# Seven block products of a hybrid layer in another order: three copied by ScalarE and three sums on VectorE instead of one and five, one block summed by TensorE

## The chip, the cores and the metric

The kernel runs on one core of one Trainium2 chip. The metric is the device time of one execution in microseconds (us); the kernel before has a median of 2258.8 us over three runs (2258.38 to 2259.35). A lower time is better.

## What is computed

All data are FP32. A residual stream `x` of 1024 tokens by 512 goes through four layers, each with a layer norm ahead of it and an addition to `x` behind it:

```python
x = x + block_sparse_linear(layernorm(x))   # 512 x 512, 32x32 blocks masked
x = x + ffn(layernorm(x))                   # silu(x Wg) * (x Wu) @ Wd, int4-like weights, 1792 wide
x = x + mixer(layernorm(x))                 # state-space mixer, 2 sequences of 512 tokens
x = x + ffn(layernorm(x))                   # the same FFN again
```

In the mixer an input projection gives a gate `g` and an inner signal `x`, each 8192 wide, the shared matrices B and C (8 groups, 128 wide each) and a step size `dt` for each of 128 heads. A causal convolution of 4 taps and SiLU follow for `x`, B and C. A chunked scan computes, for each head, a masked score matrix times the inputs inside a chunk of 128 tokens, and the states carried from chunk to chunk. The result plus a skip term is normalised by its mean square, multiplied by SiLU(g) and projected back to 512.

## The kernel before, in words

**Products of two by two blocks.** Every large projection is cut into 2x2 blocks: two tiles of 128 output channels by two halves of 512 tokens, with the 512 inputs in two halves. Four output blocks of 128x512 would need eight block products; a scheme of the Strassen-Winograd kind does with seven. `left_sides` (L166) makes sums of the weights (`s1`, `s2`, `s3`, `s4`) on GpSimd; the sums of the activations (`t1` to `t4`) are made once for all in `tq` and in `xn_t` (L152 to L164; `last_quarter`, L164, overwrites a block of `xn_t` with `t3`, `third_quarter` makes `t4`).

`seven` (L177 to L227) is a Python generator with seven yields: each step issues one block product and what belongs to it, and the caller issues other work between the steps. One block product is the inner function `product` (L185): two FP32 matmuls of 128x128 by 128x512, of which TensorE (PE in the profile) runs two passes each, so four entries in the trace. The four output blocks are sums of the seven products. Part of a sum is made by TensorE itself, which adds a product to what already stands in a PSUM bank; part is made on VectorE (DVE), from a bank and an SBUF tile. Three PSUM banks, `x`, `y` and `z`, serve one `seven`. The order before is:

1. `x = a11 b11`; ScalarE (ACT) copies it to an SBUF tile, `c21` (L202).
2. `y = s2 t2`; DVE: `c12 = c21 + y` (L206).
3. `z = s1 t1`.
4. `y += s3 t3` on TensorE; DVE: `c22 = c21 + y` (L211), `c22 += z` (L212); output (1,1).
5. `x += a12 b21` on TensorE; output (0,0) straight from the bank.
6. `y += a22 t4`; DVE: `c21 + y` (L220); output (1,0).
7. `z += s4 b22`; DVE: `c12 + z` (L225); output (0,1).

With `in_place` the last two sums are written back into their bank, where `done` reads them. There are 96 such calls: 24 in the two FFNs (gate with tag `proj`, up with tag `yo`; `done` is a SiLU on ACT or a multiply on DVE), 32 in `x_front` (`proj`, in place; `done` is `conv`, which puts one ACT instruction, L732, and three DVE taps, L735, into a list that `drain` issues later), 8 in `group` (B and C of a group, in place, `done` again `conv`), and 32 in `g_front` (not in place; `done` only notes the tile, and its SiLU, L750, comes later as "later").

**Phases of the mixer.** The 64 channel tiles go two at a time through phases `ph` 1 to 32. A phase projects the tiles of the next step (`x_front`, then `g_front`), transposes the present ones (`tokens`: `x_tr` on PE, L828, and the product `x_dt` on DVE, L832), computes the scores of heads (`half_scores` and `back_scores`, each eight pieces a phase: four Relu, L893, an Exp, L900, an Exp, L903, all ACT; then a multiply by `gm` on DVE, L901, which waits in a list until `flush`; and a multiply on GpSimd, L907), the states (`both_states`), the scan (`half_scan`: `py` on PE, L920 and L929; the skip term L940 and the gating L943 on DVE) and projects an older phase back (`outs`, L957 with the sum L969; half of it by another scheme of seven products, `out_seven`, L1022 with the sum L1035). `squares` (L949 on ACT, L950 on GpSimd) collects the mean square. Seven of the 32 phases (3, 7, ... 27) also call `group` for new B and C; in those `g_front` uses only `proj` banks, elsewhere ("proj", "yo", "yo"). Ahead of phase 1 lies a set-up, written out by hand, with the first `x_front`, the step sizes (`step_sizes`), the cumulative sums (`decays`: `pacs`, `pa`, `pl`), the first group and the first `g_front`.

**What sets the order.** The order of the program is the order on PE, ACT and DVE; nothing reorders these queues. An instruction that waits holds up all behind it on its engine. GpSimd (POOL) and the DMA queue of SyncE (SP) follow the order of a scheduler. PSUM has three banks `proj`, three `yo`, two `tr`; the next owner of a bank waits for the last reader of the old one.

Of the kernel before, what the change touches and what calls it, by code (L numbers as in the profile page):

```python
# [27 lines left out]
CTG = NCT // G  # L28
# [5 lines left out]
PP = 2  # L34
# [3 lines left out]
def kernel(  # L38
# [138 lines left out]
    def seven(left, tag, tmp, done, in_place):  # L177


        a11, a12, s3, a22, s1, s2, s4 = left  # L180
        b11, t3, b21, b22, t1, t2, t4 = right

        def product(ps, a, b, start, stop):
            for kc in range(KH):
                nc.tensor.matmul(  # L185
                    ps,
                    lhsT=a[:, kc, :],
                    rhs=b[:, kc, :],
                    start=(start and kc == 0),
                    stop=(stop and kc == KH - 1),  # L190
                    skip_group_check=True,
                )

        tags = [tag] * 3 if isinstance(tag, str) else tag

        def bank(i):
            return psum.tile([P, SEQ], F32, tag=tags[i], name=f"{tags[i]}{i}", bufs=3)

        x = bank(0)
        c12, c21, c22 = tmp(0, 1), tmp(1, 0), tmp(1, 1)  # L200
        product(x, a11, b11, True, False)
        nc.scalar.copy(c21, x)  # L202
        yield
        y, z = bank(1), bank(2)
        product(y, s2, t2, True, False)
        nc.vector.tensor_add(c12, c21, y)  # L206
        yield
        product(z, s1, t1, True, False)
        yield
        product(y, s3, t3, False, False)  # L210
        nc.vector.tensor_add(c22, c21, y)  # L211
        nc.vector.tensor_add(c22, c22, z)  # L212
        done(1, 1, c22)
        yield
        product(x, a12, b21, False, True)
        done(0, 0, x)
        yield
        product(y, a22, t4, False, True)
        r = y if in_place else c21
        nc.vector.tensor_add(r, c21, y)  # L220
        done(1, 0, r)
        yield
        product(z, s4, b22, False, True)
        r = z if in_place else c12
        nc.vector.tensor_add(r, c12, z)  # L225
        done(0, 1, r)
        yield  # L227

    def stir(n):
# [440 lines left out]
    def mixer(waiting, step_args, loaded):  # L670

        with ExitStack() as st:
# [69 lines left out]
            def drain(n=None):  # L742

                n = len(taps) if n is None else min(n, len(taps))
                for f in taps[:n]:
                    f()
                del taps[:n]

            def silu(dst, src):
                nc.scalar.activation(dst, src, AF.Silu)  # L750
# [15 lines left out]
            def group_scores(made, shared, bs=range(2)):  # L766
                for b in bs:
                    b_t, c_t = made[b]
                    b_tok = grp.tile([P, NCH - 1, P], F32, tag=f"b_tok{b}", name="b_tok", bufs=1)
                    pt = psum.tile([P, NCH - 1, P], F32, tag="tr", name="b_tr")  # L770
                    for c in range(NCH - 1):
                        nc.tensor.transpose(pt[:, c, :], b_t[:, c * P : (c + 1) * P], ident)
# [8 lines left out]
                    shared.append((c_t, b_tok, gm))  # L781

            units = [(j, b) for j in range(PP) for b in range(2)]

# [301 lines left out]
            last_quarter()  # L1086
            third_quarter()
            next(steps)
            next(steps_dt)
            next(steps)  # L1090
            next(steps)
            next(steps_dt)
            drain(3)
            next(steps)
            next(steps)
            run(steps)
            exps = decays(1)
            groups[0] = []
            ces = []
            steps_bc, made = group(0, wbc, "yo")  # L1100
            next(steps_bc)
            exps()
            half_scores(0, 0, heads, ces)
            drain(3)
            next(steps_bc)
            drain(3)
            half_scores(1, 0, heads, ces)
            next(steps_bc)
            next(steps_bc)
            drain(3)  # L1110
            half_scores(2, 0, heads, ces)
            next(steps_bc)
            next(steps_bc)
            run(steps_bc)
            gate, later = g_front(wg, gts)
            next(gate)
            half_scores(3, 0, heads, ces)
            drain(3)
            next(gate)
            drain(3)  # L1120
            next(gate)
            for u in units:
                silu(xcs[u], xcs[u])
            next(gate)
            drain(3)
            for x in (*made[0], made[1][1]):
                silu(x, x)
            run(gate)
            for f in ces:
                f()  # L1130
            for dst, src in later:
                silu(dst, src)
            drain()
            silu(made[1][0], made[1][0])
            wx = load_pair(NCT + PP, NCT + PP + 1)


# [17 lines left out]

            for ph in range(1, n_ph + 1):
                front, last = ph < n_ph, ph >= 2
                if not front:

                    units = [(j, b) for b in range(2) for j in range(PP)]  # L1160
# [43 lines left out]
                mid = last and not final  # L1204
                if final:

                    gate_q = weights()
# [7 lines left out]
                tokens(1)  # L1215
                if made and last:
                    drain()
                    silu(made[1][0], made[1][0])
                if mid:
                    outs7 = out_seven(lefts, rights, ph == 2)  # L1220

# [15 lines left out]
                    next(steps)  # L1237
                    flush()
                    both_states(0)
                    o()  # L1240
                    next(steps)
                    o()
                    next(steps)
                    drain(3)
                    o()
                    back_scores(4)
                    next(steps)
# [52 lines left out]
                    for u in units:  # L1300
                        silu(xcs_new[u], xcs_new[u])
                    flush()
                    next(gate)
                    if not new_group:
                        drain(3)
                    run(gate)
                else:
                    next(steps)
                    if not last:
                        group_scores(made, groups[0], [0])  # L1310
                    else:
                        merge(1)
                    next(steps)
                    if not last:
                        group_scores(made, groups[0], [1])
                        made = None
                        flush()
                    else:
                        back_scores(2)
# [6 lines left out]
                        merge(3)  # L1326
                        back_scores(3)
                    next(steps)
                    flush()
                    if not last:  # L1330
                        back_scores(4)
                    both_states(0)
                    next(steps)
                    drain(3)
                    next(steps)
                    run(steps)
# [60 lines left out]
                    half_scores(1, c0, heads_new)  # L1397
                    if last:
                        next(gate)
                        for u in units:  # L1400
                            silu(xcs_new[u], xcs_new[u])
                        next(gate)
                    drain(3)
                    if last:
                        flush()
                    if final:
                        next(gate)
                        ups[0]()
                    run(gate)
                if not new_group:  # L1410
# [2 lines left out]
                    silu(dst, src)  # L1413
                if made:

                    for x in (*made[0], made[1][1]):
                        silu(x, x)
                    groups[(c0 + PP) // CTG] = []
                gts_old, gts, xcs, heads = gts, gts_new, xcs_new, heads_new


# [203 lines left out]
```

## Time and profile before

| | before |
|---|---|
| median of 3 runs | 2258.8 us (2258.38 to 2259.35) |
| profiled execution, span | 2256.4 us |
| granted clock of TensorE | 1.000 |
| ACT copies at L202 | 96, 564 to 613 ns |
| DVE sums at L206, L211, L212, L220, L225 | 5 x 96, 672 to 697 ns |

The profiled execution's span is 2.4 us under the median of the runs: it runs from the first to the last instruction and leaves out what lies around it. "Busy" is the share of the span in which an engine works; for an engine that does nothing but follow another it says little. The table of waits names who sat idle, for which instruction, and who ended it.

### The profile page before, as it was taken

The page shows a single profiled execution, that of the slowest core. Times are in us where ns is not written, and L with a number is a line of the kernel's source. Part 1 is how long each engine was busy: PE and PEld are TensorE (multiplying, and loading weights), DVE is VectorE, ACT ScalarE, POOL GpSimd, SP SyncE. Part 2 cuts the span into 40 slices and gives each one's busy share as a digit, 9 for nine tenths or more (in the row PEclk, how much of TensorE's full clock was granted, in tenths as well). Part 3 has the DMA queues.
Part 4 walks back from the last instruction along what each step waited for, and adds up shares of the span by engine and source line. Part 5 has one row for each costly group of instructions (what it writes and reads, how often), then busy time and mean ns, then how long its engine had stood idle before and what let it go on. Part 6 is the DMA issues. An engine that isn't in the chain of part 4 may idle for free.

```text
span 2256.4 us, 29331 instructions
## 1 busy us (share of the span) xinstructions
PE 2241.1 (99%) x10356; PEld 1340.5 (59%) x10356; DVE 1766.8 (78%) x3017; ACT 1166.2 (52%) x2474; POOL 1193.9 (53%) x1202
## 2 busy tenths in 40 slices
PE   9999999999999999999999999999999999999999
PEld 5445875556665665665566656656655666544468
DVE  5456558888888888888888888888888989865552
ACT  4111056756665665666566656656665665731100
POOL 3765023655655566566556555665665564536610
PEclk9999999999999999999999999999999999999999
DMA  6563021222222222222222222221222322337500
GB/s 196 191 202 108 24 70 61 80 66 76 74 69 73 76 75 85 65 77 82 66 77 70 71 75 74 77 84 60 82 76 67 111 66 75 122 103 232 196 10 28
DMA packets 145779, 201.53 MB, mean 89 GB/s; under 512 B 7136, under 2 KB 92000, under 8 KB 145632
## 3 DMA queue, kind: packets, MB, share of 16 engines
q1 hardware_dynamic: 145056, 198.61, 27.7%
q8 instruction: 82, 1.34, 0.2%
q10 hardware_dynamic: 576, 1.05, 0.1%
q14 instruction: 65, 0.53, 0.1%
HBM read 194.91 MB, written 4.72 MB: 88 GB/s over the span
## 4 chain that ended last, share of the span: by engine, by line
PE 95%; DVE 3%; ACT 1%; issue 0%; POOL 0%; DVEq 0%; ACTq 0%; POOLq 0%
PE proj L185 31%; PE yo L185 19%; PE po L957 11%; PE po L1022 8%; PE ffn_o L557 7%; PE py L920 5%; PE pst L849 4%; PE py L929 4%; PE x_tr L828 2%; PE pg L487 1%; PE bs_o L336 1%; PE pu L487 1%; PE pgm L779 1%; DVE xc L735 1%; PE ln_tr L142 0%; PE stir L233 0%
## 5 line engine op out<-in xcount | busy, mean ns | idle before, releaser
L907 POOL TENSOR_TENSOR ce<-ce,c_t 128x384 f32<-128x384 f32 x256 | 288.5, 1131 | 318.3 <-ACT ce L903 312.6
L185 PE MATMUL proj<-xn_t,w 128*128 128x512 f32 x824 | 384.6, 593 | 2.0 <-DVE gt L206 1.7
L893 ACT ACTIVATE m<-bc,acs 128x128 f32<-128x128 f32 x1024 | 324.8, 389 | 6.8 <-PE py L920 5.8
L185 PEld LDWEIGHTS proj<-xn_t,w 128*128 128x128 f32 x824 | 153.0, 190 | 155.8 <-issue 146.3
L957 PE MATMUL po<-wo,gt 128*128 128x512 f32 x528 | 238.2, 599 | 0.4 <-DVE y L940 0.4
L171 POOL TENSOR_TENSOR ws<-w 128x256 f32<-128x256 f32 x96 | 74.0, 771 | 308.7 <-DMA w<-in_win_t_dram 269.9
L901 DVE TENSOR_TENSOR m<-m,gm 128x512 f32<-128x512 f32 x256 | 227.6, 907 | 11.3 <-ACT m L900 10.4
L735 DVE SCALAR_TENSOR_TENSOR xc<-proj,cw,xc 128x511 f32<-128x511 f32 (+2 forms) x288 | 214.6, 746 | 6.6
L950 POOL TENSOR_TENSOR sq_acc<-sq_acc,y 128x512 f32<-128x512 f32 x128 | 175.8, 1377 | 76.7 <-ACT y L949 76.5
L185 PE MATMUL proj<-tq,ws 128*128 128x512 f32 x432 | 199.2, 592 | 0.0
L920 PE MATMUL py<-m,x_dt 128*64 128x128 f32 x2048 | 181.4, 276 | 0.1
L900 ACT ACTIVATE m<-m 128x512 f32<-128x512 f32 x256 | 161.3, 630 | 7.4
L957 PEld LDWEIGHTS po<-wo,gt 128*128 128x128 f32 x528 | 96.3, 190 | 109.7 <-issue 103.9
L185 PE MATMUL yo<-tq,ws 128*128 128x512 f32 x336 | 153.4, 599 | 0.4 <-ACT acs L715 0.4
L185 PE MATMUL yo<-xn_t,w 128*128 128x512 f32 x328 | 151.0, 592 | 0.0
L929 PE MATMUL py<-ce,state 128*64 128x128 f32 x1536 | 149.7, 273 | 0.0
L920 PEld LDWEIGHTS py<-m,x_dt 128*64 128x64 f32 x2048 | 122.5, 137 | 30.0 <-issue 14.4
L949 ACT ACTIVATE y<-y 128x512 f32<-128x512 f32 x128 | 76.5, 623 | 110.3 <-DVE gt L943 110.3
L969 DVE TENSOR_TENSOR x_sb<-x_sb,po 128x512 f32<-128x512 f32 x136 | 92.9, 685 | 48.9 <-PE po L957 47.2
L903 ACT ACTIVATE ce<-bc 128x384 f32<-128x384 f32 x256 | 129.8, 507 | 0.0
L245 POOL TENSOR_TENSOR w<-w,sf 128x1024 f32<-128x1024 f32 (+1 forms) x30 | 70.0, 2335 | 112.9 <-DVE w L244 87.2
L732 ACT ACTIVATE xc<-proj,cb,cw 128x512 f32<-128x512 f32 x96 | 74.2, 775 | 105.8 <-DVE proj L225 76.6
(229 smaller groups left out, 4491.7 us busy)
## 6 DMA issues: line engine op xcount, KB each, us to landing
bc<-acs_d SPq DMA_DIRECT2D x128, 512.0 KB, 3.8
w<-in_win_t_dram SPq DMA_DIRECT2D x64, 512.0 KB, 3.8
wo<-in_wo_t_dram SPq DMA_DIRECT2D x31, 512.0 KB, 4.0
wi<-in_down_w_dram SPq DMA_DIRECT2D x14, 512.0 KB, 3.9
zi<-in_down_z_dram SPq DMA_DIRECT2D x14, 512.0 KB, 4.7
sf<-in_down_s_dram SPq DMA_DIRECT2D x14, 512.0 KB, 4.3
wi<-in_gate_w_dram SPq DMA_DIRECT2D x13, 512.0 KB, 4.2
zi<-in_gate_z_dram SPq DMA_DIRECT2D x13, 512.0 KB, 5.3
```

What stands on the lines that cost most here:

```text
L185: nc.tensor.matmul(ps, lhsT=a[:, kc, :], rhs=b[:, kc, :], start=(start and kc == 0), stop=(stop and kc == KH - 1), skip_group_check=True,)
L557: nc.tensor.matmul(ps, lhsT=a[:, k, :], rhs=b(k), start=(start and k == 0), stop=(stop and k == KF - 1), skip_group_check=True,)
L735: nc.vector.scalar_tensor_tensor(dst[:, s:], ps[:, : SEQ - s], cw[:, t, 3 - s : 4 - s], dst[:, s:], ALU.mult, ALU.add)
L893: nc.scalar.activation(m[:, c, :], bc[:, hh, c * P : (c + 1) * P], AF.Relu, bias=acs[:, t, h : h + 1], scale=-1.0,)
L900: nc.scalar.activation(m, m, AF.Exp, scale=-1.0)
L901: mults.append(lambda: nc.vector.tensor_mul(m, m, shared[b][2]))
L907: nc.gpsimd.tensor_mul(ce, ce, c_t[:, P:].rearrange("p (c l) -> p c l", l=P))
L920: nc.tensor.matmul(py[hh * HD : (hh + 1) * HD, c * P : (c + 1) * P], lhsT=x_dt[:, c, hh, :], rhs=m[:, c, :], start=True, stop=(c == 0),)
L929: nc.tensor.matmul(py[hh * HD : (hh + 1) * HD, c * P : (c + 1) * P], lhsT=state[:, c - 1, hh, :], rhs=ce[:, c - 1, :], start=False, stop=True,
L950: nc.gpsimd.tensor_add(sq_acc[:, b, :], sq_acc[:, b, :], y)
L957: nc.tensor.matmul(po, lhsT=gts[j, b][:, c * P : (c + 1) * P], rhs=wo[:, j, :], start=(j == 0), stop=(j == PP - 1),)
L1022: nc.tensor.matmul(banks[k][:, c, :], lhsT=a[:, t], rhs=b, start=(start and c == 0), stop=stop, skip_group_check=True,)
```

## The change

The seven products stand in a new order with other sums:

1. `y = a11 b11`; ACT copies it to `m1`.
2. `z = s1 t1`; ACT copies it to `m3`.
3. `y += s2 t2` on TensorE; ACT copies the sum to `u2`.
4. `z += s4 b22`; DVE: `u2 + z`; output (0,1).
5. `y += s3 t3`; DVE: `m3 += y`; output (1,1).
6. `x = a12 b21`; DVE: `m1 + x`; output (0,0).
7. `y += a22 t4` on TensorE; output (1,0) straight from the bank.

So one copy and five sums become three copies and three sums; the number of products is the same. A product that adds to a bank must wait until the copy of that bank is done: 3 for `m1`, 4 for `m3`, 5 for `u2`; and 7 must wait for the sum of 5, which reads the same bank. The callers are fitted to the new order of outputs: some steps, drains, scores, squares and SiLUs stand elsewhere, and the list of a group's tiles becomes a dictionary, since B and C of the second sequence now come first.

```diff
-        x = bank(0)
-        c12, c21, c22 = tmp(0, 1), tmp(1, 0), tmp(1, 1)
-        product(x, a11, b11, True, False)
-        nc.scalar.copy(c21, x)
+        y = bank(0)
+        m1, m3, u2 = tmp(1, 0), tmp(1, 1), tmp(0, 1)
+        product(y, a11, b11, True, False)
+        nc.scalar.copy(m1, y)
         yield
-        y, z = bank(1), bank(2)
-        product(y, s2, t2, True, False)
-        nc.vector.tensor_add(c12, c21, y)
+        z = bank(1)
+        product(z, s1, t1, True, False)
+        nc.scalar.copy(m3, z)
         yield
-        product(z, s1, t1, True, False)
+        product(y, s2, t2, False, False)
+        nc.scalar.copy(u2, y)
+        yield
+        product(z, s4, b22, False, True)
+        r = z if in_place else u2
+        nc.vector.tensor_add(r, u2, z)
+        done(0, 1, r)
         yield
         product(y, s3, t3, False, False)
-        nc.vector.tensor_add(c22, c21, y)
-        nc.vector.tensor_add(c22, c22, z)
-        done(1, 1, c22)
+        nc.vector.tensor_add(m3, m3, y)
+        done(1, 1, m3)
         yield
-        product(x, a12, b21, False, True)
-        done(0, 0, x)
+        x = bank(2)
+        product(x, a12, b21, True, True)
+        r = x if in_place else m1
+        nc.vector.tensor_add(r, m1, x)
+        done(0, 0, r)
         yield
         product(y, a22, t4, False, True)
-        r = y if in_place else c21
-        nc.vector.tensor_add(r, c21, y)
-        done(1, 0, r)
-        yield
-        product(z, s4, b22, False, True)
-        r = z if in_place else c12
-        nc.vector.tensor_add(r, c12, z)
-        done(0, 1, r)
+        done(1, 0, y)
         yield
...
             next(steps)
+            next(steps)
             next(steps_dt)
             next(steps)
             next(steps)
             next(steps_dt)
+            next(steps)
             drain(3)
-            next(steps)
-            next(steps)
             run(steps)
...
             steps_bc, made = group(0, wbc, "yo")
             next(steps_bc)
             exps()
-            half_scores(0, 0, heads, ces)
             drain(3)
             next(steps_bc)
             drain(3)
-            half_scores(1, 0, heads, ces)
             next(steps_bc)
+            half_scores(0, 0, heads, ces)
             next(steps_bc)
             drain(3)
-            half_scores(2, 0, heads, ces)
             next(steps_bc)
+            half_scores(1, 0, heads, ces)
             next(steps_bc)
             run(steps_bc)
             gate, later = g_front(wg, gts)
             next(gate)
-            half_scores(3, 0, heads, ces)
+            half_scores(2, 0, heads, ces)
             drain(3)
             next(gate)
             drain(3)
             next(gate)
+            half_scores(3, 0, heads, ces)
+            drain()
+            next(gate)
+            next(gate)
             for u in units:
                 silu(xcs[u], xcs[u])
-            next(gate)
-            drain(3)
-            for x in (*made[0], made[1][1]):
+            for x in (*made[1], *made[0]):
                 silu(x, x)
             run(gate)
...
-                all_squares()
+                if not mid:
+                    all_squares()
...
                     next(steps)
+                    all_squares()
                     tokens(2)
                     tokens(3)
                     flush()
                     o()
                     next(steps)
-                    back_scores(2)
+                    back_scores(1 if ph == 2 else 2)
                     o()
                     o()
-                    back_scores(3)
+                    if ph > 2:
+                        back_scores(3)
                     next(steps)
                     flush()
...
                         for i, _ in enumerate(steps):
-                            if i in (1, 3, 5):
+                            if i in (1, 2, 5):
                                 drain(3)
...
                     half_scores(0, c0, heads_new)
                     next(gate)
                     drain(3)
+                    next(gate)
                     half_scores(1, c0, heads_new)
                     next(gate)
                     next(gate)
@@
                     flush()
-                    next(gate)
                     if not new_group:
                         drain(3)
                     run(gate)
```

In phases 1 and 31 `group_scores`, `flush` and `half_scores(1)` move by a step in the same manner.

More of the change, by code (lines that the diff above doesn't have):

```diff
@@ L780, in group_scores @@
                     nc.vector.tensor_tensor(gm, pg, tri.unsqueeze(1).to_broadcast([P, NCH, P]), ALU.mult)
-                    shared.append((c_t, b_tok, gm))
+                    shared[b] = (c_t, b_tok, gm)
             units = [(j, b) for j in range(PP) for b in range(2)]
@@ L1092, in mixer @@
             next(steps_dt)
+            next(steps)
             drain(3)
-            next(steps)
-            next(steps)
             run(steps)
             exps = decays(1)
-            groups[0] = []
+            groups[0] = {}
             ces = []
@@ L1132, in mixer @@
                 silu(dst, src)
-            drain()
-            silu(made[1][0], made[1][0])
             wx = load_pair(NCT + PP, NCT + PP + 1)
@@ L1157, in mixer @@
                 front, last = ph < n_ph, ph >= 2
+                mid = last and ph < n_ph - 1
                 if not front:
@@ L1203, in mixer @@
                 final = ph == n_ph - 1
-                mid = last and not final
                 if final:
@@ L1217, in mixer @@
                     drain()
-                    silu(made[1][0], made[1][0])
+                    silu(made[0][1], made[0][1])
                 if mid:
@@ L1232, in mixer @@
                     next(steps)
-                    back_scores(2)
+                    back_scores(1 if ph == 2 else 2)
                     o()
                     o()
-                    back_scores(3)
+                    if ph > 2:
+                        back_scores(3)
                     next(steps)
                     flush()
+                    if ph == 2:
+                        back_scores(2)
                     both_states(0)
@@ L1241, in mixer @@
                     next(steps)
+                    if ph == 2:
+                        back_scores(3)
                     o()
@@ L1244, in mixer @@
                     drain(3)
+                    if ph == 2:
+                        flush()
                     o()
@@ L1309, in mixer @@
                     if not last:
-                        group_scores(made, groups[0], [0])
+                        group_scores(made, groups[0], [1])
                     else:
@@ L1314, in mixer @@
                     if not last:
-                        group_scores(made, groups[0], [1])
+                        group_scores(made, groups[0], [0])
                         made = None
@@ L1328, in mixer @@
                     next(steps)
-                    flush()
                     if not last:
+                        flush()
                         back_scores(4)
@@ L1333, in mixer @@
                     next(steps)
+                    if last:
+                        flush()
                     drain(3)
@@ L1396, in mixer @@
                     drain(3)
-                    half_scores(1, c0, heads_new)
                     if last:
+                        next(gate)
+                        half_scores(1, c0, heads_new)
+                        next(gate)
                         next(gate)
@@ L1401, in mixer @@
                             silu(xcs_new[u], xcs_new[u])
-                        next(gate)
                     drain(3)
@@ L1406, in mixer @@
                     if final:
-                        next(gate)
                         ups[0]()
@@ L1414, in mixer @@
                 if made:
-                    for x in (*made[0], made[1][1]):
+                    for x in (*made[1], made[0][0]):
                         silu(x, x)
-                    groups[(c0 + PP) // CTG] = []
+                    groups[(c0 + PP) // CTG] = {}
                 gts_old, gts, xcs, heads = gts, gts_new, xcs_new, heads_new
```

## Prediction

> **What bounds the kernel now.** First the page: busy times, TensorE's clock and the chain that ended last.
>
> ```profile
> span 2256.4 us, 29331 instructions
> ...
> PE 2241.1 (99%) x10356; PEld 1340.5 (59%) x10356; DVE 1766.8 (78%) x3017; ACT 1166.2 (52%) x2474; POOL 1193.9 (53%) x1202
> ...
> PEclk9999999999999999999999999999999999999999
> ...
> PE 95%; DVE 3%; ACT 1%; issue 0%; POOL 0%; DVEq 0%; ACTq 0%; POOLq 0%
> ```
>
> PE works 99% of the span at full clock, and 95% of the chain is its own work. The count of PE instructions stays (seven products are seven products), so the change can only take away or add moments in which PE waits. Next come the waits of PE, longest first (us in total, times, longest):
>
> ```profile
> PE ln_tr L142 <- ACT tmp L127: 3.0, 2, 1.6
> PE proj L185 <- DVE tmp L211: 1.9, 1, 1.9
> PE proj L185 <- DVE gt L206: 1.7, 1, 1.7
> ...
> PE b_tr L772 <- ACT b_t L750: 1.1, 1, 1.1
> ...
> PE yo L185 <- ACT acs L715: 0.4, 1, 0.4
> ```
>
> The first is the layer norm at the start, which the change doesn't touch. The others happen once each, and their times (timeline of PE) are 417, 387, 359 and 333 us: set-up and first two phases. The steady phases show none. The start-to-start distances of PE's rows, less the usual distance of that pair, say the same: between 319 and 430 us they exceed it by 8.5 us in all, and from 434 to 1890 us only by single excesses of 0.1 us. One restart behind a stall costs 0.10 us over the wait itself (the row after it starts 0.53 us later instead of 0.43). **The most that can be won is 8.5 us.**
>
> **Work that moves and costs nothing.** 96 sevens each lose two sums and gain two copies. Their rows (behind the first bar: busy us in all, mean ns of one; behind the second: idle time of the engine before them and who ended it):
>
> ```profile
> L202 ACT COPY gt<-proj 128x512 f32<-128x512 f32 x32 | 18.4, 574 | 31.7 <-PE proj L185 31.5
> L202 ACT COPY tmp<-proj 128x512 f32<-128x512 f32 x32 | 18.2, 568 | 0.0
> ...
> L206 DVE TENSOR_TENSOR tmp<-tmp,proj 128x512 f32<-128x512 f32 x32 | 22.0, 688 | 29.1 <-PE proj L185 26.9 <-ACT tmp L202 2.0
> ```
>
> 192 x 0.688 = 132 us leave DVE, 192 x 0.574 = 110 us come to ACT. All of it lies beside PE, which neither engine holds up in the steady phases: nothing of the 132 us is on the path. If DVE were the bound, it would be worth more than 100 us. The Trainium skill ("Perfetto Trace Analysis", Optimizing Scalar/DVE Operations) advises to hand work of a saturated DVE to ScalarE; by it these 132 us would be the gain. DVE is at 78% here and PE doesn't wait for it, so by the row the gain is nothing.
>
> **The new waits.** Products 3, 4 and 5 add to a bank that ACT copies; each has one other product, 4 x 0.43 = 1.72 us, between it and the product that was copied. A copy starts 0.04 us after the visible end of its product, lasts 0.57 and lets PE go 0.06 later; the visible end is 0.16 behind the slot, so it is done 0.84 us into these 1.72. If ACT is free there is no stall, 0.9 us to spare. That is the case of all 24 sevens of the FFNs, where ACT has little else: 0. [...] By the row nothing is paid wherever ACT is free.
>
> Where ACT isn't free, what stands ahead of the copy counts. So I laid the queues out by hand, per stage, in the new program order with the durations above.
>
> **New-group phases (7).** (a) Product 3 of the group must wait for the copy of product 1, which stands behind a square, which waits for a gating on DVE. This is the timeline of before at that place (897 to 903 us):
>
> ```profile
> 897.88 0.74 DVE L943 SCALAR_TENSOR_TENSOR gt<-y,nw,gt 128x512 f32<-128x512 f32 x1
> ...
> 898.65 0.63 ACT L949 ACTIVATE y<-y 128x512 f32<-128x512 f32 x1 [3.72 <-DVE gt L943]
> ...
> 899.19 0.57 ACT L202 COPY tmp<-yo 128x512 f32<-128x512 f32 x1
> ...
> 899.59 0.19 PEld L185 LDWEIGHTS yo<-tq,ws 128*128 128x128 f32 x1 [0.24 <-issue]
> ```
>
> The copy ends at 899.76, +0.06 = 899.82; the third product wants to start at 899.59: 0.23 + 0.10 = 0.33 us. Before, that product used another bank and didn't care. The gating can't come earlier, as the DVE sum ahead of it at 896.35 waits for PE itself. (b) In the same phase product 4 of `g_front` must wait for the copy `m3` of product 2, which now stands behind `half_scores(0)`:
>
> ```profile
> 915.81 0.51 ACT L903 ACTIVATE ce<-bc 128x384 f32<-128x384 f32 x1
> 916.23 1.27 ACT L893 ACTIVATE m<-bc,acs 128x128 f32<-128x128 f32 x4
> ```
>
> The copy takes the place of the row at 916.23, ends at 916.80, and releases PE at 916.86; the slot is 916.72: 0.14 + 0.10 = 0.25 us. Together 0.58 x 7 = **+4.1 us**. Bounds: 0, if ACT comes 0.25 us earlier in both; 7 us, if the pair costs 1.0.
>
> **Ordinary phases (22).** In `x_front` the scores of `back_scores(2)` and (3) come behind the copy `m3`, so behind product 2: at 1029.1 us in the phase that begins at 1023.3, where before they start at 1026.24. Two half scores with a table load (1.28) last 5.8 us (1026.24 to 1032.1 before); then comes `u2`, done at 1035.5; product 5, which needs it, has its slot at 1036.67: 1.1 us to spare. Narrower is the transpose `tokens(3)` on PE, which needs the `tr` bank that `x_dt` of `tokens(1)` (L832, DVE) reads. Its slot is 1025.43. Before, the x_dt ends at 1024.68; after, `half_scores(1)` stands one product later, so its multiply does too, and I get 1025.11: 0.32 us to spare. No stall: **0**. If this cover is gone, see the second rival.
>
> **Set-up, phases 1 and 2.** The 8.5 us go: the wait for `t3` (0.56 us at 321; product 4 is now `s4 b22`, which needs neither `t3` nor `t4`), the wait for `acs` (0.70), for `b_t` (1.27; it is finished earlier, since B and C of the second sequence come first), for `gt` at 387 (1.98, one sum less ahead), for `tmp` at 417 (2.20), for y at 428 (0.62), and some tenths. What comes in their place: `pacs` needs the step sizes. The Ln of these and its table load stand behind the copy `u2` (product 3 ends at 320.8), and then come 1.28 + 0.63, Exp with its load 1.9, and four DVE rows, 3.2 us: 328.6 against a slot of 327.6, +1.1. In the group, product 7 waits for the sum of 5 behind a drain, +0.4. In `g_front`, product 4 waits for `m3` behind `half_scores(2)`, +0.9. The transposes at 365 keep their 0.5. In phase 1 product 7 of `g_front` waits for the sum of 5, +0.3 (instead of 2.0). In phase 2 product 3 waits for `m1`, which stands behind the SiLUs of the gate and a table load, +1.2; `outs(3)` +0.4. Sum 4.8; 4.8 - 8.5 = **-3.7 us**. Here the queues are full and each term has an error of some tenths; bounds -7 and 0.
>
> Phase 31: product 4 of `g_front` waits 0.3 us for `m3` behind `half_scores(0)`, and a stall of the same size at 1921 us goes: 0. The tail has no seven of another kind. Sum: 2256.4 + 4.1 - 3.7 = 2256.8 us of span. The median of the runs is 2.4 us above the profiled span: **2259.2 us**.
>
> **Rivals.** *Faster:* the waits of the set-up go as priced or better (-3.7 to -7), and the two waits of the new-group phases don't bite, because their 0.23 and 0.14 us are smaller than the error of a hand-made layout: 2256.4 + 2.4 - 3.7 = 2255.1 down to 2251.8. For it: the page's ACT is only 52% busy. Against: both waits hang on rows that another engine fixes.
>
> *Slower:* one mechanism, the `tr` bank of `tokens(3)` in the 22 ordinary phases. The multiply L901 of the last scores lasts 0.68 us when POOL is idle (1021.00, two in 1.28 us), and 1.0 to 1.48 beside POOL's multiplies (1030.98 and 1032.29). As the scores come later, POOL's `ce` products come later too and may meet it. With two multiplies at 1.0, DVE is 0.64 us later, the spare 0.32 is gone and PE loses 0.32 + 0.10 = 0.42 us a phase: 22 x 0.42 = 9.2 us, 2268.4. It decides from 0.32 us per phase on. Two at 1.4 would be 22 x 1.2 = 27 us; I hold this unlikely, since POOL rests from 1020 to 1025 in before.
>
> *No effect:* the changed waits are all covered, and what goes in the set-up is eaten by other waits there: 2258.8.
>
> **Chances.** Forecast with its own spread, and no effect, both within 0.2% (4.5 us, about what a measurement can tell from no change): 0.42. The faster rival beyond 2254.3: 0.29. The slower one, or new-group waits of twice the price, beyond 2263.3: 0.29. The range takes in the faster rival's low end and most of the slower: 2252 to 2268.
>
> **What would show it.** In the changed profile: DVE busy down by about 130 us, ACT up by about 110. PE busy the same. Waits "yo<-ACT tmp" and "proj<-ACT gt" at the copies, seven times each, 0.1 to 0.3 us long; none in ordinary phases. The waits at 387 and 417 us gone, new ones before `pacs` and in phase 2. Phase length stays 48.2 us (ordinary) and grows from 62.6 to 63.2 (new group). I'm wrong if `x_tr` or `proj` waits stand 20 times or more in the table, or if the first scan of phase 2 starts not earlier than before.

## The result and the profile after

The changed kernel is slower: median 2272.9 us (2272.4 to 2275.5, four runs) against 2258.95 of the kernel before; ratio 1.0065, 95% interval 1.0051 to 1.0079, so +14 us. The forecast was 2259.2, the range ended at 2268.

The page after, lines of busy time and of the chain that ended last:

```profile
span 2273.7 us, 29415 instructions
...
PE 2247.1 (99%) x10356; PEld 1338.0 (59%) x10356; DVE 1656.2 (73%) x2825; ACT 1278.5 (56%) x2666; POOL 1201.0 (53%) x1202
...
PE 76%; DVE 16%; ACT 7%; issue 1%; DMA 0%; SPq 0%; DVEq 0%; ACTq 0%
```

DVE lost 111 us of busy time (forecast: about 130), ACT gained 112, PE's count is the same: the work moved as intended. But the chain, which was 95% PE, now runs through DVE for 16% and ACT for 7%. An engine at 73% busy has come onto the path. The table of PE's waits (total, times, longest) says where:

```profile
PE yo L185 <- ACT tmp L202: 7.3, 7, 1.2
PE po L958 <- DVE y L941: 4.8, 8, 0.9
...
PE po L958 <- DVE x_sb L1034: 1.3, 1, 1.3
...
PE po L1023 <- POOL sums L1004: 0.8, 1, 0.8
...
PE pacs L703 <- DVE acs L667: 0.7, 1, 0.7
PE proj L185 <- ACT gt L206: 0.6, 1, 0.6
```

Two rows count seven or eight: one per new group. The table counts from the visible end of the matmul ahead, which lies 0.16 us behind the slot of the next; a wait of 0.56 us there costs 0.72, and 0.83 with the restart. I set the start of the same transposes (`x_tr`, L828 before, L829 after) of both traces side by side. The first FFN keeps its distance; an ordinary phase adds 0.00 us; a new-group phase adds 1.5 to 1.7 us (the fifth of the seven only 0.9), the phase behind it 0.83 us (once 1.27, with a wait for `gm`); set-up and the first two phases win 1.5 us; phase 31 wins 0.25. This profiled execution is also the longest of its four runs (2275.46 us): up to 14 us, ahead of all that the change touches, it lost 2.15 us, 1.7 of them from 11 to 14 us, where TensorE was granted half its clock. That is no effect of the change, and the other three runs take 2272.4 to 2272.9 us. It also shifts the set-up by some tenths: in the profiles of e1, e2, e4 and e5, which have the set-up of the changed kernel but not that start, the set-up wins 2.4 us.

**The stall in a new-group phase.** The place shown in the prediction, now at 5.9 us later: DVE's rows ahead of the group's first copy, then ACT's, then PE's.

```profile
897.73 1.49 DVE L902 TENSOR_TENSOR m<-m,gm 128x512 f32<-128x512 f32 x1
...
900.56 1.48 DVE L902 TENSOR_TENSOR m<-m,gm 128x512 f32<-128x512 f32 x1
...
902.56 1.16 DVE L902 TENSOR_TENSOR m<-m,gm 128x512 f32<-128x512 f32 x1
...
904.24 0.68 DVE L902 TENSOR_TENSOR m<-m,gm 128x512 f32<-128x512 f32 x1
904.84 0.74 DVE L944 SCALAR_TENSOR_TENSOR gt<-y,nw,gt 128x512 f32<-128x512 f32 x1
```

```profile
905.62 0.63 ACT L950 ACTIVATE y<-y 128x512 f32<-128x512 f32 x1 [4.32 <-DVE gt L944]
906.15 0.57 ACT L202 COPY tmp<-yo 128x512 f32<-128x512 f32 x1
```

```profile
903.79 1.88 PE L185 MATMUL yo<-tq,ws 128*128 128x512 f32 x4
906.87 1.52 PE L185 MATMUL yo<-tq,ws 128*128 128x512 f32 x3 [1.19 <-ACT tmp L202]
```

Gating, square, copy, product 3: the chain is the one that the prediction named. But the gating starts 1.04 us later than in before (904.84 against 897.88 + 5.92), because the four multiplies ahead of it take 4.81 us and not 3.25 (before: 0.68, 0.68, 0.89, 1.00; some of the 1.56 us is made up, as DVE had 0.43 us of idle time among them). They run beside GpSimd's products, and these come later since GpSimd first makes the group's weight sums (L171 to L174), which wait for their transfer. GpSimd's first sum and its products in after:

```profile
894.67 0.73 POOL L171 TENSOR_TENSOR ws<-w 128x256 f32<-128x256 f32 x1 [3.70 <-DMA w<-in_win_t_dram]
...
897.67 2.41 POOL L908 TENSOR_TENSOR ce<-ce,c_t 128x384 f32<-128x384 f32 x2
```

In before the first sum starts at 886.20, so it is 2.55 us later than the shift of 5.92, and the products came singly there, with pauses of 1.1 to 1.3 us. The transfer's row on SP's queue, in before and in after:

```profile
882.19 0.92 SPq L611 DMA_DIRECT2D w<-in_win_t_dram  x2
```

```profile
890.70 0.93 SPq L612 DMA_DIRECT2D w<-in_win_t_dram  x2
```

Less the 5.92 us, that is 2.59 us later. Of the two weight tiles, the one that the transfer fills is `x_front`'s. Before, its last reader was product 6 (`a22 t4`; product 7 read the sum `s4`, which lies in another tile). In the new order `a22 t4` is product 7: one product of 1.72 us and one step of the output scheme, 0.86 us, later. The step that the diff shows least, which product comes last, sets when a buffer is free.

### The profile page after: what moved, and what is told of

Its sections match the earlier page's. It is cut to its first block, busy times and chain, and to the rows that moved or that the text cites. A ratio compares the mean times of both kernels' runs of the same rounds, so it can differ in the third digit from the quotient of the medians.

```text
span 2273.7 us, 29415 instructions
## 1 busy us (share of the span) xinstructions
PE 2247.1 (99%) x10356; PEld 1338.0 (59%) x10356; DVE 1656.2 (73%) x2825; ACT 1278.5 (56%) x2666; POOL 1201.0 (53%) x1202
## 4 chain that ended last, share of the span: by engine, by line
PE 76%; DVE 16%; ACT 7%; issue 1%; DMA 0%; SPq 0%; DVEq 0%; ACTq 0%
PE proj L185 27%; PE yo L185 14%; PE po L958 8%; PE ffn_o L558 7%; PE py L921 4%; PE po L1023 4%; DVE xc L736 3%; PE py L930 3%; DVE m L902 2%; DVE state L864 2%; PE pst L850 2%; ACT m L894 2%; PE x_tr L829 2%; DVE x_sb L1036 2%; PE bs_o L337 1%; PE pg L488 1%
## 5 line engine op out<-in xcount | busy, mean ns | idle before, releaser
L908 POOL TENSOR_TENSOR ce<-ce,c_t 128x384 f32<-128x384 f32 x256 | 276.6, 1088 | 251.6 <-ACT ce L904 247.5
L902 DVE TENSOR_TENSOR m<-m,gm 128x512 f32<-128x512 f32 x256 | 222.1, 880 | 86.7 <-ACT m L901 86.7
L185 PE MATMUL proj<-tq,ws 128*128 128x512 f32 x520 | 240.7, 592 | 0.0
L736 DVE SCALAR_TENSOR_TENSOR xc<-proj,cw,xc 128x511 f32<-128x511 f32 (+2 forms) x288 | 214.0, 745 | 6.7
L837 POOL TENSOR_TENSOR x_dec<-x_dt,dec 128x384 f32<-128x384 f32 x128 | 122.2, 969 | 161.4 <-DVE x_dt L833 125.5
L171 POOL TENSOR_TENSOR ws<-w 128x256 f32<-128x256 f32 x96 | 74.4, 775 | 202.6 <-DMA w<-in_win_t_dram 192.9
L185 PEld LDWEIGHTS proj<-tq,ws 128*128 128x128 f32 x520 | 98.4, 190 | 98.1 <-issue 92.2
L1036 DVE TENSOR_TENSOR x_sb<-x_sb,po 128x512 f32<-128x512 f32 x170 | 115.9, 682 | 47.6 <-PE po L1023 47.6
L185 PE MATMUL proj<-tq,w 128*128 128x512 f32 x304 | 143.1, 593 | 0.0
```

The costliest lines, as they stand in the source:

```text
L185: nc.tensor.matmul(ps, lhsT=a[:, kc, :], rhs=b[:, kc, :], start=(start and kc == 0), stop=(stop and kc == KH - 1), skip_group_check=True,)
L736: nc.vector.scalar_tensor_tensor(dst[:, s:], ps[:, : SEQ - s], cw[:, t, 3 - s : 4 - s], dst[:, s:], ALU.mult, ALU.add)
L902: mults.append(lambda: nc.vector.tensor_mul(m, m, shared[b][2]))
L908: nc.gpsimd.tensor_mul(ce, ce, c_t[:, P:].rearrange("p (c l) -> p c l", l=P))
L1036: nc.vector.tensor_add(q, q, banks[k])
```

## Experiments

Each kernel was timed beside the kernel before, which ran at 2258.2 to 2259.0 us there. **Theory A**: DVE is late, since the scores come later on ACT. **Theory B**: DVE is late in new-group phases, since the weights come late and GpSimd gets in its way. **Theory C**: only the place of the copy in ACT's queue counts.

### e1: the squares behind the group's first product

```diff
-                    all_squares()
+                    if not new_group:
+                        all_squares()
...
                         for i, _ in enumerate(steps):
+                            if i == 0:
+                                all_squares()
```

> In new-group phases the squares are issued behind the group's first product and its copy, not ahead of them. Theory A (DVE is late at the end of a phase, because the scores came later, and the copy m1 inherits it through gating and square): the seven stalls at product 3 of the group (1.2 to 1.4 us each) go, about -9 us against the changed kernel, near 2264 us; the 0.8 us wait for y in the phase after stays. Theory C (only the copy's place in ACT's queue matters, DVE's lateness has no other victim): also -9. If less than -5 comes, what is late is found again further on (product 4 of the group, or g_front).

Measured: 2263.35 us (ratio 1.0022, 1.0012 to 1.0031), 9.5 below the changed kernel. All seven stalls at product 3 went, the waits for y stayed. So the place of some 9 us is known; why DVE is late there is not, since A, B and C all allow this result.

### e2: the scores ahead of x_front's second product

```diff
+                    if ph > 2:
+                        back_scores(2)
                     next(steps)
-                    back_scores(1 if ph == 2 else 2)
+                    if ph == 2:
+                        back_scores(1)
```

> back_scores(2) goes ahead of the second product of x_front again, so that it doesn't stand behind the copy m3. Theory A: DVE no longer idles 3.2 us for the exponentials, so it is on time at the end of the phase: the 0.8 us wait for y (7 times) goes, and the stall at product 3 of the group falls from 1.3 to 0.3 or less: -10 to -14 us, near 2260 us. Theory B (the weights of the group arrive 2.6 us later, because x_front's last reader of its weight tile is now product 7, so GpSimd's sums and products meet DVE's multiplies): only the wait for y goes, product 3 still stalls by 0.8 or more: -5 to -8, near 2266.

Measured: 2273.2 us (1.0049 to 1.0079): nothing won. The stall at product 3 is 1.2 to 1.5 us, the wait for y 0.65 in place of 0.73. Both theories missed the wait for y; the stall is as B says. A falls in this form: in the phase behind a new group ACT is still behind with the SiLUs of B and C, and two scores and two copies take as long in either order (DVE's second multiply ends only 0.1 us earlier than in the changed kernel).

### e4: a weight tile of its own for the group

```diff
-                    common.append(weights(True).rearrange("p kc j c -> p (kc j c)")[:, : 2 * DH].rearrange("p (t n) -> p t n", n=DH))
+                    common.append(sc.tile([P, 2, DH], F32, name="common"))
...
-                    wbc = load_group((c0 + PP) // CTG)
+                    ct = 2 * NCT + (c0 + PP) // CTG
+                    w = weights(True)
+                    for j, c in enumerate((ct, ct + G)):
+                        nc.sync.dma_start(
+                            w[:, :, j, :], win_t[:, c * P : (c + 1) * P].rearrange("(kc p) c -> p kc c", p=P)
+                        )
+                    wbc = left_sides(w)
```

`common`, a buffer of `out_seven`, moves to a tile of its own, so the third weight tile is free for the group.

> The weights of a new group get a tile of their own, so that their transfer doesn't wait for x_front's product 7. Theory B: GpSimd's sums come earlier, DVE's four multiplies ahead of the gating fall from 4.8 to about 3.3 us, and the stall at product 3 of the group falls from 1.3 to about 0.3: -7 us, near 2266. Theory A: the stall stays within 0.3 us of 1.3, 2271 to 2273.

Measured: 2266.2 us (ratio 1.0033, 1.0020 to 1.0047), 6.7 below the changed kernel, as B said. DVE's multiplies at the same place:

```profile
892.44 0.68 DVE L902 TENSOR_TENSOR m<-m,gm 128x512 f32<-128x512 f32 x1
...
894.82 0.68 DVE L902 TENSOR_TENSOR m<-m,gm 128x512 f32<-128x512 f32 x1
...
896.02 0.89 DVE L902 TENSOR_TENSOR m<-m,gm 128x512 f32<-128x512 f32 x1
...
897.59 1.00 DVE L902 TENSOR_TENSOR m<-m,gm 128x512 f32<-128x512 f32 x1
```

They are those of before, row by row (GpSimd's sums end at 881.58 here, long ahead of them), and a new-group phase now adds 0.62 us in all: 0.39 at product 3, 0.23 at product 4 of `g_front`. This is what the prediction had for the two (0.33 and 0.25). So about 1.0 us of the 1.4 at product 3 goes with the late transfer; over the seven phases the stall falls from 9.0 to 2.8 us.

### e10: the squares of the other phases behind the scores

```diff
                     next(steps)
-                    all_squares()
+                    if ph == 2:
+                        all_squares()
...
                     if ph > 2:
                         back_scores(3)
+                        all_squares()
```

> The changed kernel, with nothing but the squares of the phases that aren't new-group moved behind back_scores(3); the group's copy stays behind its square. The wait for y goes (7 times 0.83 us, -5.8): 2267. Theory B says that the stall at product 3 of the group stays at 1.2 to 1.4 us, since it comes from the multiplies beside GpSimd, which begin when TensorE frees the sum ahead of them. Theory A says that it shrinks to 0.3 to 0.6 as DVE is less late: 2261.

Measured: 2269.2 us (ratio 1.0049, 1.0034 to 1.0064), 3.7 below the changed kernel. The waits for y are gone, but the stall at product 3 of the group is still there, 1.4 to 1.5 us: less lateness from the phase before doesn't help it, as B said. In the first two of these phases it even grew by 0.1 to 0.2 us, in the fifth, which lost only 0.7 us in the changed kernel, by 0.8, and the group's score products wait 0.9 us for `gm` once (751 us; 0.3 in the changed kernel): so 2267 was missed by 2.

### e5 and e6: what makes y late

e5 is e1, e2 and e10 together; e6 is e1 and e10, with the scores behind product 2.

> The squares behind the group's first product (as in e1), back_scores(2) ahead of x_front's second product (as in e2), and in the other phases the squares behind back_scores(3). Theory A, in the form that e2 left (ACT has too much ahead of the scores at the start of a phase: the two copies and two squares, so DVE idles some 3.5 us for the exponentials and is late for y): the multiplies come 1 to 2 us earlier than in e1, the seven waits of 0.83 us for y go: -5.8 against e1, 2257.6 us, which is about the kernel before. Rival D (y is late because of DVE's own work, a tap of 1.38 us beside GpSimd among it): the waits stay above 0.4 us, 2261 or more.

> As e5, but back_scores(2) stays behind x_front's second product, so only the squares are moved. Theory A says that the scores then still start behind the copy m3, which waits for product 2: the multiplies move little, the waits for y stay at 0.5 to 0.83 us: 2261 to 2263.5. If it is as fast as e5, the squares alone were to blame.

Measured: e5 2258.65 us (ratio 0.9991 to 1.0010), e6 2258.97 (0.9992 to 1.0011): 4.7 and 4.4 below e1, the waits for y gone in both. The place of the scores doesn't matter, the two squares do, and rival D falls: the tap is still there and the waits are gone. Why, from the phase behind a new group. The changed kernel, ACT and then DVE:

```profile
936.65 0.57 ACT L202 COPY tmp<-proj 128x512 f32<-128x512 f32 x1
937.12 1.15 ACT L950 ACTIVATE y<-y 128x512 f32<-128x512 f32 x2
938.17 0.58 ACT L206 COPY tmp<-proj 128x512 f32<-128x512 f32 x1
```

```profile
941.89 1.08 DVE L902 TENSOR_TENSOR m<-m,gm 128x512 f32<-128x512 f32 x1 [2.04 <-ACT m L901]
944.13 1.03 DVE L902 TENSOR_TENSOR m<-m,gm 128x512 f32<-128x512 f32 x1 [1.16 <-ACT m L901]
```

and DVE in e6, which at this place is 8.34 us ahead of the changed kernel:

```profile
932.82 0.69 DVE L902 TENSOR_TENSOR m<-m,gm 128x512 f32<-128x512 f32 x1 [1.31 <-ACT m L901]
935.06 0.69 DVE L902 TENSOR_TENSOR m<-m,gm 128x512 f32<-128x512 f32 x1 [1.55 <-ACT m L901]
```

ACT has no gap in the first fence; copies and squares, 2.0 us, stand ahead of the scores. DVE idles 3.2 us for the exponentials, and from 945 us on it has no more gap until y, which PE awaits. In e6 the multiplies end 1.07 us earlier: 0.73 by the earlier start of the second and 0.34 by its length (0.69 for 1.03). That covers the 0.73 us wait (0.83 with the restart). In the changed kernel the second multiply starts 1.9 us later than in before, so the squares are 0.7 of these; the other 1.2 us, with the two copies among them, don't reach y alone. No run takes the copies out.

### e8: late weights in the kernel before

```diff
+        product(z, s4, b22, False, True)
+        r = z if in_place else c12
+        nc.vector.tensor_add(r, c12, z)
+        done(0, 1, r)
+        yield
         product(y, a22, t4, False, True)
         r = y if in_place else c21
         nc.vector.tensor_add(r, c21, y)
         done(1, 0, r)
-        yield
-        product(z, s4, b22, False, True)
-        r = z if in_place else c12
-        nc.vector.tensor_add(r, c12, z)
-        done(0, 1, r)
         yield
...
```

The callers change only in which SiLU of a group comes last, since another block is finished last.

> The kernel before, with its products 6 and 7 exchanged, so that the weight tile's last reader is product 7 as in the changed kernel; the copies and sums are those of before. Theory B says that the group's weights come about 2.6 us later, and that DVE's four multiplies ahead of the gating take some 4.8 us instead of 3.25. No product waits there for the copy behind the square, so TensorE should lose nothing by it: within 1.5 us of the kernel before. If it is slower by 4 us or more, late weights cost by themselves.

Measured: 2268.7 us (ratio 1.0043, 1.0028 to 1.0058), +10. The mechanism is there: the four multiplies take 1.52, 1.48, 1.15 and 0.68 us, together 4.83. That it would cost nothing was wrong: the sum L206 stands behind the late gating on DVE, and product 4 of the group waits for it (0.30 us at 904.73; six such waits, 2.1 us with their restarts). The larger part has nothing to do with the weights. Product 6 is now `z += s4 b22`, and it must not write the bank z before DVE has read it for the sum L212 behind product 4; before, z was written one product later. The first FFN shows it, DVE and then PE's weight load for product 6:

```profile
80.88 0.69 DVE L212 TENSOR_TENSOR sg<-sg,proj 128x512 f32<-128x512 f32 x1
```

```profile
81.62 0.30 PEld L185 LDWEIGHTS proj<-xn_t,ws 128*128 128x128 f32 x2 [0.61 <-DVE sg L212]
```

In 66 of the 96 calls this load starts 0.05 to 0.12 us behind the end of L212, and there product 6 loses 6.5 us in all (0.14 us a call in the FFNs); in the other 30 it loses nothing. 6.5 and 2.1 us are 8.6 of the 9.6 us by which the last product of the trace comes later. So e8 shows that late weights lengthen the multiplies in the kernel before too, and its 10 us are no price of late weights: that price is e4's.

### e3 and e3b: the new order with the callers of before

The function `seven` of after in the kernel before. e3 applies the SiLU of one C block ahead of that block's last taps, so it computes that block differently; e3b puts it behind.

> The new order of products alone: the callers are those of the kernel before, except for which SiLU of a group comes last and the list that became a dictionary. Theory A and B: the same lateness, since the callers' scores stand behind the second product in both: 2270 to 2280 us. If it is faster than the changed kernel, the refit of the callers did harm; if slower, it helped by the difference.

> As e3, the new order of products in the callers of the kernel before; here the SiLU of the block whose taps come last (C of the first sequence) is also put last, which e3 left in its old place, ahead of that block's last taps. Both theories expect the time of e3 within 3 us, 2346 to 2352 us; another time would say that e3's place of the SiLU mattered.

Measured: 2349.3 (e3) and 2350.4 us (e3b; ratio 1.0409, 1.0393 to 1.0424). The range of 2270 to 2280 was far off: without the refit of the callers the new order costs 92 us, and the refit wins back 78. The largest row of its waits is product 7, which must not write before DVE has read the bank for the sum of product 5:

```profile
PE proj L185 <- DVE gt L217: 44.2, 30, 2.1
```

It shows in 30 of 32 `g_front`s. In an ordinary phase the callers, made for the old order, put three taps (L736) and two multiplies (L902) on DVE between the sums L213 and L217:

```profile
569.35 0.69 DVE L213 TENSOR_TENSOR gt<-gt,yo 128x512 f32<-128x512 f32 x1 [1.07 <-PE yo L185]
569.96 2.31 DVE L736 SCALAR_TENSOR_TENSOR xc<-proj,cw,xc 128x511 f32<-128x511 f32 x3
572.18 1.28 DVE L902 TENSOR_TENSOR m<-m,gm 128x512 f32<-128x512 f32 x2
573.38 0.68 DVE L217 TENSOR_TENSOR gt<-gt,proj 128x512 f32<-128x512 f32 x1
```

Product 7 has to wait until 574.12. In the changed kernel the taps stand ahead of L213 at this place and L217 follows it directly (558.04 and 559.69 us), and the row is gone. The row holds 44 of the 92 us; copies in the way of `g_front` and of the group (L209 5.9, L202 7.7) and single waits hold some 20 more, and the rest I have not traced. This refit, which the prediction priced as single moves, is worth more (78 us) than the changed kernel loses (14).

### e7, e9 and e11: the last wait of g_front

All are e5 with `half_scores(0)` of new-group phases moved: behind product 2 (e7), behind product 3 (e9), or cut, so that product 2 and its copy are issued between its two Exps (e11):

```diff
                 mults.append(lambda: nc.vector.tensor_mul(m, m, shared[b][2]))
+                if hooks:
+                    next(hooks.pop())
...
                     if new_group:
                         next(gate)
+                    if new_group:
+                        hooks.append(gate)
                     half_scores(0, c0, heads_new)
-                    next(gate)
+                    if not new_group:
+                        next(gate)
...
```

`next(hooks.pop())` issues product 2 of `g_front` and its copy.

> As e5, and in new-group phases half_scores(0) comes behind product 2 of g_front and so behind the copy m3. The seven waits of 0.13 us (0.23 with the restart) at product 4 of g_front go: -1.6 us against e5, near 2256. Against it: the scores and their multiplies come 2.3 us later there, and may make DVE late for the transposes of the next phase; then nothing is won or it is lost again.

> As e5, and in new-group phases half_scores(0) comes behind product 3 of g_front, so behind both copies m3 and u2. The seven waits of 0.13 us (0.23 with the restart) at product 4 go, and the wait at product 5 that e7 got for them as well: -1.6 us against e5, near 2257. Rival: all scores of the phase come 2.3 us later, DVE or ACT is late for the transposes or the score products of the next phase, and 1 us or more is lost there: 2258.5 to 2262.

> As e5, and in new-group phases product 2 of g_front with its copy m3 is issued between the Exp of the scores (L901) and the Exp of ce, so that the copy stands one ACT row (0.42 us) earlier and the scores only 0.5 us later. The seven waits of 0.13 us (0.23 with the restart) at product 4 go: -1.6 us against e5, near 2257, which would be 1.5 us below the kernel before. Rival: the wait turns up elsewhere as in e7 and e9, 2258.5 or more.

Measured: e7 2258.84 (0.9991 to 1.0010), the wait moved from product 4 to product 5, which needs `u2`. e9 2261.07 (1.0002 to 1.0022), both gone, but seven waits of 0.4 us at the next transposes for a SiLU. e11 2256.62 us against 2259.02 of the kernel before beside it, ratio 0.999 (0.9981 to 0.9999): the wait is gone and none took its place in the new-group phases; a single wait for `gm` at 748 us is 0.8 us long (0.2 in e5). e11 is the fastest kernel here, 2.4 us below the kernel before, 16 below the changed one; the interval only just leaves out no difference.

## Why the prediction was wrong

**Right.** The 110 us that move from DVE to ACT are worth nothing by themselves. The sevens of the FFNs and the ordinary phases away from a new group cost 0.00 us, and `x_tr` never waited in them. The second wait of a new-group phase was 0.23 us (0.25 forecast), and the chain gating, square, copy, product 3 was named.

**The step that failed**: "The gating can't come earlier, as the DVE sum ahead of it at 896.35 waits for PE itself." That is so, but it can come later, and I took its time from before. Product 3 lost 1.4 us at the place shown, not 0.33, and 9.0 us in the seven phases where 2.3 were forecast; 6.2 of these go with the group's late transfer (e4: 0.39 us each). The prediction follows no DMA and nothing on GpSimd in that phase. The weight tile's last reader moved from product 6 to 7, and that moved SP's transfer, GpSimd's sums and products, and so DVE's multiplies.

**A second failed step**: the seven phases behind a new group were counted among the ordinary ones, at 0. In these, ACT starts late after the SiLUs of B and C, and the two more copies and the two squares, now behind the first product, push the scores; y is 0.83 us late with the restart, and moving the squares takes that away (e6, e10). 7 x 0.83 = 5.8 us; with a longer wait for `gm` in one of them 6.3.

**Mis-sized**: the set-up, -3.7 forecast, -2.4 measured (here and below in the profile of e1, whose set-up is that of the changed kernel). Most new waits came as priced (`pacs` 0.9 for 1.1, product 4 of `g_front` 0.8 for 0.9, product 7 of the group 0.5 for 0.4), product 3 of phase 2 was 0.3 for 1.2. Two were missed in phase 2, GpSimd's sums (L1004) at 402 us, 1.0, and DVE's copy (L1034) at 423 us, 0.9. The wait for y at 426 us, which I had go, stayed with 1.1.

Sum of the errors: new-group phases 10.5 us for 4.1, +6.4; the phases behind them +6.3; the set-up +1.3; phase 31 -0.2: 13.8. With the forecast +0.4 that is 14.2 us, against 14.0 measured.

The slower rival had the right mechanism, multiplies beside GpSimd's products, at another place (the transposes); at two multiplies of 1.4 to 1.5 us I had held it unlikely. The Trainium skill ("SBUF — State Buffer", Who interferes with whom) says that a DVE instruction with two SBUF inputs contends with a GpSimd instruction that reads SBUF. The multiply is such a one, and the rows agree: 0.68 us alone, 1.47 to 1.52 beside `ce`. The rule could have been put to the new times of both queues ahead of the run.

## What to carry to other kernels

When products, sums or copies are reordered, go through every buffer and ask who reads it last now: that reader sets the next transfer, and what the transfer releases may end on the engine that you thought idle. Times from before hold in the new order only where the releaser is unchanged; an engine that had gaps to lose in one kind of phase may have none in the phase behind it. A cheap copy is late by all that stands ahead of it in its queue: put work that nobody awaits, like these squares, behind it. PSUM banks have last readers too: product 7 in e3b and product 6 in e8 wait for a sum that still reads their bank.

## What I had not expected of the hardware

A wait of PE can cost more than itself. In e3b a wait of 3.3 us for a copy ends at 414.1 us; two windows behind it (stretch in us, its length, busy time of PE, weight loads, DVE, ACT and POOL, then the granted clock, the DMA share and GB/s):

```profile
413.50:416.00 2.50, 1.87 (x4) 0.97 (x5) 0.00 (x0) 2.48 (x8) 2.36 (x2) 0.91 0.00 0
...
417.00:418.00 1.00, 1.00 (x6) 1.00 (x6) 0.29 (x1) 0.99 (x4) 0.00 (x0) 0.50 0.00 0
```

The clock is half from about 415.6 to 419 us, so it falls more than a us behind the wait's end, and some 1.7 us are lost (matmuls that start every 0.11 us elsewhere start every 0.21 us there). In the same run a wait of 2.6 us that ends at 325.6 us is followed by 0.50 from 328 to 330 us, with starts 0.85 us apart in place of 0.43, and again 1.7 us lost. The start of the changed kernel's profiled run is a third case: PE was busy for 29 and 40% of the microseconds from 7 to 9, and the clock was 0.50 from 11 to 14 us. The Trainium skill ("TensorE: Matmul & The Clock Gate", Part 1: The HAM clock gate) says that the gate falls to half after at least one idle window of about 3.4 us, and that the window runs freely. Both waits of e3b are shorter than that, so in this run the clock fell without a window that was idle from end to end.
